# Reading the first layer's shifted copies straight from a padded input, and running its first unit of filters one image at a time

## The chip, the cores and the metric

The kernel runs on one core of one Trainium2 chip. The metric is the device time of one execution in microseconds (us). A core has five engines that run side by side, each in its own program order: TensorE (PE, matrix products; PEld is its weight load), VectorE (DVE), ScalarE (ACT), GpSimd (POOL) and SyncE (SP, which here only issues DMA transfers). They wait for one another through semaphores.

## The reference, cut to what matters

The input x has shape (4, 32, 32, 16): four images, 32x32 positions, 16 channels. Four layers follow, each adding its result to x:

```python
x = x + conv(gn(x), M0, W0, G0)          # layer 0
x = x + conv(gn(x), M1, W1, G1)          # layer 1
x = x + interval(gn(x), ...)             # layer 2, not touched here
x = x + conv(gn(x), M3, Wp3, G3)         # layer 3

def gn(v, G=8, eps=1e-5):                # groups of 2 channels, over the whole image
    g = v.reshape(B, H, W, 8, 2)
    m = mean(g, axis=(1, 2, 4)); s = var(g, axis=(1, 2, 4))
    return ((g - m) / sqrt(s + eps)).reshape(v.shape)

def conv(v, M, W, G):                    # G: (32, 32, 3, 3, 16, 16): own 3x3 filters per position
    first   = einsum('ijyx,byxc->bijc', M, v)
    shifted = conv3x3(v, kern)           # 1024 positions x 16 filters, each over the whole image
    diff    = relu(v[:, None, None] - shifted)
    second  = einsum('ijyx,bijyxc->bijc', W, diff)
    return first - second
```

For every position (i, j) and filter f a 3x3 convolution over 16 channels is made of the whole image, and what comes out is weighted and summed. The 1024 positions are eight chunks of 128; in a chunk, one filter and one image are one *step*: 128 outputs (positions of the chunk) times 1024 pixels, with 9 x 16 = 144 products each. The nine shifts (taps) of the image, 16 channels each, are the rows of the right-hand operand; they are spread over three *slots*: slot 0 holds taps 0 to 3, slot 1 taps 4 to 7, slot 2 tap 8. The upper and the lower half of the image lie in partitions 0 to 63 and 64 to 127.

The convolution is linear in its input, but the padding must be zero after the normalization, not before it.

## The kernel before: the parts that are touched

The four images are two groups of two (`GB` = 2). Phases run over (group 0, layer 0), (group 1, layer 0), (group 0, layer 1) and so on, six in all; while a phase runs, a generator `behind` slips the next phase's preparation between its steps. Instructions go to the engines in the order in which they are written.

The input of a phase is prepared by `before_conv`: normalize, transpose to channels on partitions, write to a padded image `xs` in device memory, read back 24 shifted copies.

```python
def group_norm(g, name, dst):            # on X[g]: 128 positions x 8 x 32 (image, channel)
    part = sums(X[g]) ; yield 2          # DVE
    m = mean_of(part) ; yield 1          # PE, a product with a constant matrix
    ...                                  # subtract, square, sum, PE, ACT sqrt, DVE reciprocal
    nc.vector.tensor_tensor(dst, xc, rstd, mult); yield 2

def before_conv(g, layer):
    yield from group_norm(g, f"c{g}{layer}", xn)
    ...                                  # two PE transposes of xn, ACT copy to xt
    for t in range(4):                   # xt -> xs, the padded image in device memory
        (nc.scalar if t % 2 else nc.sync).dma_start(inner[:, t], xt[...])
    yield 2
    for slot, row, tap in [(2, row, 8) for row in range(4)] + [(tap // 4, tap % 4, tap) for tap in range(8)]:
        for h in range(2):
            off = (HI * h + tap // 3) * HP + tap % 3
            r0 = 64 * h + C * row
            (nc.scalar, nc.sync)[at % 2].dma_start(          # 16 partitions x 2 images x 542
                im[g][r0 : r0 + C, slot, :, :RUN], xsv[:, :, off : off + RUN])
            at += 1
    yield 9
    halve(im9[g], im[g][:, 2], low_x)        # ACT: slot 2 rounded for the tap-8 product
    yield 2
    halve_rest(im9[g], im[g][:, 2], low_x)   # DVE
```

The weights come in *units* of eight filters (1.5 MB each, tile `raw`, four buffers). `prep` subtracts 1 from one tap's weight (so that the step yields shifted minus v) on POOL and makes the slot-2 weights `W9` on ACT; `prep_rest` finishes `W9` on DVE.

```python
load_raw(0); load_chunk(0)               # first instructions of the program, after the load of X[0]
...
start = before_conv(*phases[0]); ...     # all of it runs before the first step
prep(0); prep_rest(0)

def conv_layer(phase, behind):
    for t in range(NT):                  # 8 chunks
        for f in range(C):               # 16 filters
            u = n * NU + f // FU         # unit of eight filters
            if f % FU == 1: prep(u + 1); load_raw(u + 3)
            if f % FU == 4: prep_rest(u + 1)
            if f == 2: load_chunk(n + 1)
            for b in range(GB):          # 2 images: one step each
                ps = bank_pair(...)      # PSUM, three pairs of banks
                for slot in range(3):
                    for h in range(2):
                        nc.tensor.matmul(ps[:, h, :], lhsT=w[:, f % FU, :], rhs=v[:, :, :H], ...)
                nc.vector.scalar_tensor_tensor(junk, ps, 0.0, chunks[n], op0=min, op1=mult,
                                               accum_out=acc[...])
                wait -= 1
                if wait <= 0: wait = next(behind, 1 << 20)

def behind(phase):
    if phase == 0:
        load_raw(1); load_raw(2)
        nc.scalar.dma_start(X[1], x[1]); zeros(1); yield 1
        yield from constants()
    ...                                  # before_conv of the next phase, first_term
    if phase == 0: yield from first_term(g, layer)
```

Of the kernel before, what the change touches and what calls it, by code (L numbers as in the profile page):

```python
# [8 lines left out]
F32 = mybir.dt.float32  # L9
F32R = mybir.dt.float32r  # L10
AF = mybir.ActivationFunctionType
ALU = mybir.AluOpType
AX = mybir.AxisListType

P = 128
B, H, C = 4, 32, 16
NG = 2
GB = B // NG
GC = GB * C
NL = 3  # L20
NP = H * H
NT = NP // P
HP = H + 2
# [11 lines left out]


@with_exitstack
def net_kernel(ctx: ExitStack, tc: tile.TileContext, x, convs, iv_w, iv_b, out):

# [16 lines left out]
    def bank_pair(name):  # L58
        return psum.tile([P, 2, 512], F32, tag="ps", name=name)

    def bank(name):
        return psum.tile([P, 512], F32, tag="one", bufs=2, name=name)
# [3 lines left out]
    n_chunks = len(phases) * NT  # L66

    X = [const.tile([P, NT, GC], F32, name=f"X{g}") for g in range(NG)]
    nc.scalar.dma_start(X[0], x[0])


    raws, units, chunks = {}, {}, {}
# [1 line left out]
    def load_raw(u):  # L74
        if u < n_chunks * NU:
            n = u // NU
            raws[u] = wpool.tile([P, 3, FU, P], F32, tag="raw", bufs=4, name=f"raw_{u}")
            nc.sync.dma_start(raws[u], convs[phases[n // NT][1]][2][n % NT, u % NU])

    def load_chunk(n):  # L80
        if n < n_chunks:
            t = n % NT
            chunks[n] = wpool.tile([P, NP], F32, tag="WT", name=f"WT_{n}")
            nc.sync.dma_start(chunks[n], convs[phases[n // NT][1]][1][t * P : (t + 1) * P, :])

    load_raw(0)
    load_chunk(0)


    mean_w = const.tile([P, P], F32, name="mean_w")  # L90
# [19 lines left out]
    def halve(dst, src, mask):  # L110
        nc.scalar.activation(dst, src, AF.Copy, scale=mask[:, 1:2])  # L111

    def halve_rest(dst, src, mask):
        nc.vector.scalar_tensor_tensor(  # L114
            dst, src, mask[:, 0:1], dst.bitcast(F32), op0=ALU.mult, op1=ALU.add
        )
# [1 line left out]
    xs = [dram.tile([GC, NPP], F32, name=f"xs{g}") for g in range(NG)]  # L118
    zero = const.tile([P, HP], F32, name="zero")
    xt = [const.tile([P, 2, ROWS, HP], F32, name=f"xt{g}") for g in range(NG)]  # L120
    im = [const.tile([P, 3, GB, PITCH], F32, name=f"im{g}") for g in range(NG)]
    im9 = [const.tile([P, GB, PITCH], F32R, name=f"im9{g}") for g in range(NG)]

    def zeros(g):

        nc.gpsimd.memset(xt[g], 0.0)
        nc.gpsimd.memset(im[g][:, 2], 0.0)
        for y in (0, HP - 1):
            nc.gpsimd.dma_start(xs[g][:, y * HP : (y + 1) * HP], zero[:GC])

    nc.gpsimd.memset(zero, 0.0)
    zeros(0)

    def prep(u):

        if u >= n_chunks * NU:
            return
        raw = raws.pop(u)
        f0 = u % NU * FU
        nc.gpsimd.tensor_tensor(  # L140
            raw[:, 1], raw[:, 1],
            pick[:, f0 : f0 + FU].unsqueeze(2).to_broadcast([P, FU, P]),
            ALU.subtract,
        )
        W9 = wpool.tile([P, FU, P], F32R, tag="W9", name=f"W9_{u}")
        halve(W9, raw[:, 2], low_w)
        units[u] = (raw, W9)

    def prep_rest(u):
        if u in units:  # L150
            raw, W9 = units[u]
            halve_rest(W9, raw[:, 2], low_w)

# [44 lines left out]
    def before_conv(g, layer):  # L200
        xn = work.tile([P, NT, GC], F32, tag="xn", bufs=2, name=f"xn_{g}_{layer}")
        xns[g] = xn
        yield from group_norm(g, f"c{g}{layer}", xn)

        ps = bank(f"ps_t{g}{layer}")
        for m in range(2):
            nc.tensor.transpose(  # L209
                ps[:, m * P : (m + 1) * P],  # L210
                xn[:, 4 * m : 4 * m + 4, :].rearrange("p t m -> p (t m)"),
                ident,
            )
        yield 1
        nc.scalar.copy(
            xt[g][:, :, :, 1 : 1 + H],
            ps[:, : 2 * P].rearrange("p (m r x) -> p m r x", m=2, x=H),
        )
        inner = xs[g][:, HP : HP + H * HP].rearrange("p (m t n) -> p t m n", m=2, t=4)
        for t in range(4):  # L220
            (nc.scalar if t % 2 else nc.sync).dma_start(
                inner[:, t],
                xt[g][GC * t : GC * (t + 1)].rearrange("p m r x -> p m (r x)"),
            )
        yield 2
        xsv = xs[g].rearrange("(b c) n -> c b n", b=GB)
        at = 0
        for slot, row, tap in [(2, row, 8) for row in range(4)] + [
            (tap // 4, tap % 4, tap) for tap in range(8)
# [4 lines that stand above are left out]
                (nc.scalar, nc.sync)[at % 2].dma_start(  # L234
                    im[g][r0 : r0 + C, slot, :, :RUN], xsv[:, :, off : off + RUN]
                )
                at += 1
        yield 9
        halve(im9[g], im[g][:, 2], low_x)
        yield 2  # L240
        halve_rest(im9[g], im[g][:, 2], low_x)
# [215 lines left out]
    def conv_layer(phase, behind):  # L457

        g, layer = phases[phase]
        wait = 0  # L460
        imv = im[g].rearrange("p s b (y x) -> p s b y x", x=HP)
        im9v = im9[g].rearrange("p b (y x) -> p b y x", x=HP)
        acc = work.tile([P, NT, GC], F32, tag="acc", bufs=2, name=f"acc_{phase}")
        for t in range(NT):
            n = phase * NT + t
            for f in range(C):
                u = n * NU + f // FU
                if f % FU == 1:
                    prep(u + 1)
                    load_raw(u + 3)  # L470
                if f % FU == 4:
                    prep_rest(u + 1)
                if f == 2:
                    load_chunk(n + 1)
                W, W9 = units[u]
                for b in range(GB):


                    ps = bank_pair(f"pc_{n}_{f}_{b}")
                    for slot in range(3):  # L480
                        for h in range(2):
                            r = slice(64 * h, 64 * h + 64)
                            w, v = (W9[r], im9v[r, b]) if slot == 2 else (W[r, slot], imv[r, slot, b])
                            nc.tensor.matmul(  # L484
                                ps[:, h, :],
                                lhsT=w[:, f % FU, :],
                                rhs=v[:, :, :H],
                                start=slot == 0,
                                stop=slot == 2,
                            )  # L490

                    col = b * C + f
                    junk = work.tile([P, NP], F32, tag="junk", name=f"junk_{n}_{col}")
                    nc.vector.scalar_tensor_tensor(  # L494
                        junk,
                        ps.rearrange("p h n -> p (h n)"),
                        0.0,
                        chunks[n],
                        op0=ALU.min,
                        op1=ALU.mult,  # L500
                        accum_out=acc[:, t, col : col + 1],
                    )
                    wait -= 1
                    if wait <= 0:
                        wait = next(behind, 1 << 20)
            nc.vector.tensor_tensor(X[g][:, t], X[g][:, t], acc[:, t], ALU.add)  # L506
        for _ in behind:
            pass

    def behind(phase):  # L510
        g, layer = phases[phase]
        if phase == 0:
            load_raw(1)
            load_raw(2)
            nc.scalar.dma_start(X[1], x[1])
            zeros(1)
            yield 1
            yield from constants()
        if phase + 1 < len(phases):
            g1, layer1 = phases[phase + 1]  # L520
            if layer1 == 2:
                yield from interval_layer(g1)
            yield from before_conv(g1, layer1)
            yield from first_term(g1, layer1)
        if phase == 0:
            yield from first_term(g, layer)
        if phase == len(phases) - 1:
            nc.sync.dma_start(out[1 - g], X[1 - g])

    start = before_conv(*phases[0])  # L530
    next(start)
    v = ident.rearrange("p (h q c) -> p q c h", h=2, q=4)
    nc.vector.tensor_reduce(pick, v[:, 0], axis=AX.X, op=ALU.add)
    low_w = rows_mask("low_w", ident.rearrange("p (h w k) -> p w h k", h=2, w=2)[:, 1:2])
    low_x = rows_mask("low_x", ident.rearrange("p (g x k) -> p x g k", g=4, x=2)[:, 1:2])
    for _ in start:
        pass
    prep(0)
    prep_rest(0)
    for phase in range(len(phases)):  # L540
        conv_layer(phase, behind(phase))
    nc.sync.dma_start(out[1], X[1])
# [63 lines left out]
```

## Time and profile before

| | |
|---|---|
| time, median of 3 runs | 3120.36 us (3120.36 to 3121.54) |
| span in the profile | 3119.8 us |
| PE busy | 3089.7 us, 99% |
| DVE busy | 2100.3 us, 67% |
| POOL, ACT busy | 289.2 us (9%), 147.2 us (5%) |
| chain that ended last | PE 99%, DMA 1%, everything else under 0.5% each |

The profile is read as follows. The page gives each engine's busy time and the chain of work that ended last, followed back from the last instruction: at each point, what the next thing was waiting for. The timeline lists instructions in order of time (start, duration, engine, line of the kernel, operation, tile written and tiles read; in brackets how long the engine was idle before and what ended that). `pc` is the PSUM tile of a step, `junk` its evaluation on DVE, `im` the shifted copies, `raw` the weights, `ps_mc` and `ps_vc` the two small products of the group normalization. "SPq" and "ACTq" are the DMA-issuing sides of these engines. The windows view gives, for each stretch of time, the busy time of PE, PEld, DVE, ACT and POOL with instruction counts, the granted PE clock, the DMA engines' busy share and GB/s.

### The profile page before, as it was taken

The page shows a single profiled execution, that of the slowest core. Times are in us where ns is not written, and L with a number is a line of the kernel's source. Part 1 is how long each engine was busy: PE and PEld are TensorE (multiplying, and loading weights), DVE is VectorE, ACT ScalarE, POOL GpSimd, SP SyncE. Part 2 cuts the span into 40 slices and gives each one's busy share as a digit, 9 for nine tenths or more (in the row PEclk, how much of TensorE's full clock was granted, in tenths as well). Part 3 has the DMA queues.
Part 4 walks back from the last instruction along what each step waited for, and adds up shares of the span by engine and source line. Part 5 has one row for each costly group of instructions (what it writes and reads, how often), then busy time and mean ns, then how long its engine had stood idle before and what let it go on. Part 6 is the DMA issues. An engine that isn't in the chain of part 4 may idle for free.

```text
span 3119.8 us, 37923 instructions
## 1 busy us (share of the span) xinstructions
PE 3089.7 (99%) x15792; PEld 1568.0 (50%) x15792; DVE 2100.3 (67%) x3348; ACT 147.2 (5%) x159; POOL 289.2 (9%) x173
## 2 busy tenths in 40 slices
PE   6999999999999999999999999999999999999999
PEld 4444455444444444444446654444664444444444
DVE  4656666666666666666677766667776666666666
ACT  0000000000000000000000000000100000000000
POOL 2000000000000000000013300002230000000000
PEclk9999999999999999999999999999999999999999
DMA  4322111321111231211111132121113211111100
GB/s 144 123 102 75 48 68 48 125 75 66 50 62 60 69 124 48 75 48 68 48 70 52 48 118 75 48 75 48 68 48 103 97 48 70 48 72 51 67 28 2
DMA packets 32462, 215.21 MB, mean 69 GB/s; under 512 B 5665, under 2 KB 7713, under 8 KB 18465
## 3 DMA queue, kind: packets, MB, share of 16 engines
q1 hardware_dynamic: 27168, 207.02, 18.4%
q10 hardware_dynamic: 4992, 5.74, 0.9%
q8 instruction: 124, 2.03, 0.3%
q14 instruction: 50, 0.40, 0.0%
q0 software_dynamic: 128, 0.02, 0.0%
HBM read 211.64 MB, written 1.12 MB: 68 GB/s over the span
## 4 chain that ended last, share of the span: by engine, by line
PE 99%; DMA 1%; DVE 0%; ACTq 0%; issue 0%; ACT 0%
PE pc L484 97%; PE pf L255 1%; PE pfs L263 0%; DMA im<-xs 0%; PE ps_l L386 0%; DMA X<-in_x 0%; PE ps_r L397 0%; PE ps_l L384 0%; PE ps_t L209 0%; PE ps_vc L174 0%; PE ps_iv L341 0%; DMA xs<-xt 0%; PE ps_mc L174 0%; DVE xc_c L184 0%; ACTq L234 0%; DVE junk L494 0%
## 5 line engine op out<-in xcount | busy, mean ns | idle before, releaser
L484 PE MATMUL pc<-im,raw 64*128 64x512 f32 x12288 | 2920.4, 590 | 13.2 <-DMA im<-xs 13.2
L494 DVE SCALAR_TENSOR_TENSOR junk<-pc,WT 128x1024 f32<-128x1024 f32 x1536 | 1880.0, 1224 | 990.4 <-PE pc L484 986.6
L484 PEld LDWEIGHTS pc<-im,raw 64*128 64x128 f32 x12288 | 1237.2, 186 | 1137.5 <-issue 746.6
L484 PE MATMUL pc<-im,W 64*128 64x512 f32 x3072 | 1293.2, 803 | 0.0
L484 PEld LDWEIGHTS pc<-im,W 64*128 64x128 f32 x3072 | 321.1, 186 | 355.6 <-issue 343.5
L140 POOL TENSOR_TENSOR raw<-raw,pick 128x1024 f32<-128x1024 f32 x96 | 182.0, 1898 | 2278.5 <-DMA raw<-in_g 2216.9
L111 ACT ACTIVATE W<-raw,low_w 128x1024 fp32r<-128x1024 f32 x96 | 110.3, 1149 | 2198.0 <-PE pc L484 2170.1
L494 DVE DVE_READ_ACCUMULATOR junk<-pc,WT 128x1 f32 x1536 | 127.6, 83 | 0.0
L114 DVE SCALAR_TENSOR_TENSOR W<-raw,low_w,W 128x1024 fp32r<-128x1024 f32 x96 | 122.9, 1280 | 0.0
L417 POOL TENSOR_TENSOR dp_b<-ft_b,rt_r 128x1089 f32<-128x1089 f32 x16 | 39.1, 2449 | 101.6 <-ACT ft_b L410 51.5
L417 POOL TENSOR_TENSOR dp_a<-ft_a,rt_r 128x1089 f32<-128x1089 f32 x16 | 37.2, 2327 | 79.9 <-DVE s_a L424 50.2
L255 PE MATMUL pf<-MT,xn 128*32 128x512 f32 x192 | 23.1, 598 | 0.0
L424 DVE TENSOR_REDUCE s_b<-dp_b 128x33 f32<-128x1089 f32 x16 | 20.5, 1283 | 0.0
L424 DVE TENSOR_REDUCE s_a<-dp_a 128x33 f32<-128x1089 f32 x16 | 20.5, 1282 | 0.0
L114 DVE SCALAR_TENSOR_TENSOR im<-im,low_x,im 128x1088 fp32r<-128x1088 f32 x6 | 9.1, 1523 | 14.6 <-DMA im<-xs 14.6
L259 ACT COPY fs<-pf 128x512 f32<-128x512 f32 x12 | 7.0, 586 | 240.1 <-PE pf L255 240.1
L330 POOL TENSOR_SCALAR xn<-xn 128x256 f32<-128x256 f32 x2 | 1.7, 856 | 151.0 <-DVE xn L195 151.0
L506 DVE TENSOR_TENSOR X<-X,acc 128x32 f32<-128x32 f32 x48 | 13.6, 283 | 1.6
L263 PEld LDWEIGHTS pfs<-stack,fs 128*128 128x128 f32 x96 | 11.2, 191 | 3.4 <-issue 3.4
L361 DVE TENSOR_TENSOR pp<-pp 64x1024 f32<-64x1024 f32 x10 | 12.1, 1213 | 0.0
L366 DVE TENSOR_TENSOR pp<-pp 64x1024 f32<-64x1024 f32 x10 | 12.1, 1213 | 0.0
L255 PEld LDWEIGHTS pf<-MT,xn 128*32 128x32 f32 x192 | 5.0, 109 | 14.1 <-issue 14.1
(81 smaller groups left out, 160.1 us busy)
## 6 DMA issues: line engine op xcount, KB each, us to landing
raw<-in_g SPq DMA_DIRECT2D x96, 1536.0 KB, 6.6
WT<-in_w SPq DMA_DIRECT2D x48, 512.0 KB, 6.3
MT<-in_mt SPq DMA_DIRECT2D x12, 2048.0 KB, 8.3
im<-xs SPq DMA_DIRECT2D x72, 67.8 KB, 3.2
im<-xs ACTq DMA_DIRECT2D x72, 67.8 KB, 3.3
xs<-xt SPq DMA_DIRECT2D x12, 34.0 KB, 1.7
xs<-xt ACTq DMA_DIRECT2D x12, 34.0 KB, 1.8
X<-in_x ACTq DMA_DIRECT2D x2, 128.0 KB, 5.1
```

Of the source, the lines that this page charges most:

```text
L111: nc.scalar.activation(dst, src, AF.Copy, scale=mask[:, 1:2])
L114: nc.vector.scalar_tensor_tensor(dst, src, mask[:, 0:1], dst.bitcast(F32), op0=ALU.mult, op1=ALU.add)
L140: nc.gpsimd.tensor_tensor(raw[:, 1], raw[:, 1], pick[:, f0 : f0 + FU].unsqueeze(2).to_broadcast([P, FU, P]), ALU.subtract,)
L255: nc.tensor.matmul(ps[32 * j : 32 * j + 32, :], lhsT=xn[:, pt, :], rhs=mt[:, pt, :], start=pt < 4, stop=pt >= 4, tile_position=(0, 32 * j),)
L263: nc.tensor.matmul(ps[:, GC * t : GC * (t + 1)], lhsT=fs[:, t // 4, t % 4 * P : (t % 4 + 1) * P], rhs=stack, start=True, stop=True,)
L361: nc.vector.tensor_tensor(pp[k][:, :H, M:], a[:, :H, M:], a[:, s : H + s, M:], ALU.max)
L366: nc.vector.tensor_tensor(pp[k][:, :H, M:], a[:, :H, M:], a[:, :H, M - s : M - s + H], ALU.max)
L417: nc.gpsimd.tensor_tensor(t, ft[:, i, :].unsqueeze(1).to_broadcast([P, T1, T1]), rt, ALU.add,)
L424: nc.vector.tensor_reduce(s[:, i - 1, :], last, axis=AX.X, op=ALU.max)
L484: nc.tensor.matmul(ps[:, h, :], lhsT=w[:, f % FU, :], rhs=v[:, :, :H], start=slot == 0, stop=slot == 2,)
L494: nc.vector.scalar_tensor_tensor(junk, ps.rearrange("p h n -> p (h n)"), 0.0, chunks[n], op0=ALU.min, op1=ALU.mult, accum_out=acc[:, t, co ...
L506: nc.vector.tensor_tensor(X[g][:, t], X[g][:, t], acc[:, t], ALU.add)
```

## The change

Only the first phase (group 0, layer 0) is started differently. The host gives two further forms of the two images of group 0: `xq`, the same numbers as 128 partitions of 256 (for the statistics), and `xp`, channels on partitions and already padded by a ring of zeros. The 24 shifted copies are read from `xp` at the very start, before the statistics are known, and are normalized in place; where the padding has thereby become non-zero it is multiplied by zero (masks `keep_...`). The round trip over transposes and `xs` falls away for this phase. The copies, the first unit's weights and the first unit's steps are split so that image 0 and the first two filters can begin before the rest is there. The normalization of X[0] in the usual form is still needed for the first term and runs behind the steps.

```diff
-    nc.scalar.dma_start(X[0], x[0])
+    XQ = const.tile([P, 256], F32, name="XQ")
+    nc.scalar.dma_start(XQ, xq)
...
-    load_raw(0)
+    def load_copies(b, slot):                # 8 copies, 16 partitions x 542, of one image
+        for h in range(2):
+            for row in range(4):
+                tap = min(4 * slot + row, 8)
+                ...
+                (nc.scalar if h and b == 0 else nc.sync).dma_start(
+                    im[0][r0 : r0 + C, slot, b, :RUN], xpv[:, b, off : off + RUN])
+    F0 = 2
+    raws[0] = wpool.tile([P, 3, FU, P], F32, tag="raw", bufs=4, name="raw_0")
+    load_copies(0, 0)
+    nc.sync.dma_start(raws[0][:, :, :F0], convs[0][2][0, 0][:, :, :F0])
+    load_copies(0, 2)
+    load_copies(0, 1)
     load_chunk(0)
+    nc.sync.dma_start(raws[0][:, :, F0:], convs[0][2][0, 0][:, :, F0:])
+    for slot in (2, 0, 1):
+        load_copies(1, slot)
...
-            for f in range(C):
+            steps = [(f, b) for f in range(C) for b in range(GB)]
+            if n == 0:
+                steps.sort(key=lambda s: (s[0] // FU, s[1]))     # eight steps of image 0, then of image 1
+            for at, (f, b) in enumerate(steps):
-                if f % FU == 1:
+                if at % (FU * GB) == 2:
+                    load_raw(u + 3)
+                if at % (FU * GB) == (8 if u == 0 else 2):
                     prep(u + 1)
-                    load_raw(u + 3)
-                if f % FU == 4:
+                if at % (FU * GB) == (12 if u == 0 else 8):
                     prep_rest(u + 1)
...
         if phase == 0:
             load_raw(1)
             load_raw(2)
+            yield from rest_of_start()
             nc.scalar.dma_start(X[1], x[1])
...
-    start = before_conv(*phases[0])
+    pairs = ...; own = ...; to_rows = ...; to_own = ...; rows = ...      # from the identity, on DVE
+    keep = {...}                                                         # six masks, two DVE instructions each
+    s1 = sum of XQ                                # DVE
+    mean_own = to_own.T @ s1                      # PE, DVE copy
+    XQ -= mean_own; s2 = sum of XQ * XQ           # DVE
+    var = to_rows.T @ (own * s2); rstd0 = sqrt(var + eps)    # DVE, PE, ACT
+    mean0 = to_rows.T @ (own * s1); rstd0 = 1 / rstd0        # DVE, PE, DVE
+
+    def normal(eng, b, slots):
+        for slot in slots:
+            v = im[0][:, slot, b, :RUN]
+            eng.tensor_scalar(v, v, mean0[:, b : b + 1], rstd0[:, b : b + 1], op0=subtract, op1=mult)
+            ...                                   # slots 0, 1: three small multiplications by keep; slot 2: two memsets
+
+    prep(0, 0, F0)
+    normal(nc.vector, 0, [0, 2])
+    prep_rest(0, 0, F0)
+    normal(nc.gpsimd, 0, [1])
+    halve(im9[0][:, 0], im[0][:, 2, 0], low_x)
+    halve_rest(im9[0][:, 0], im[0][:, 2, 0], low_x)
+    prep(0, F0, FU)
+
+    def rest_of_start():                          # from behind(0), after the first step
+        nc.sync.dma_start(X[0], x[0])
+        prep_rest(0, F0, FU)
+        normal(nc.gpsimd, 1, [2, 0, 1])
+        yield 4
+        halve(im9[0][:, 1], im[0][:, 2, 1], low_x)
+        yield 1
+        halve_rest(im9[0][:, 1], im[0][:, 2, 1], low_x)
+        nc.gpsimd.memset(zero, 0.0)
+        zeros(0)
+        xns[0] = work.tile(...)
+        yield from group_norm(0, "c00", xns[0])
```

## The prediction, made before the changed kernel had run

> **What bounds the kernel now.** I read the page first: PE is busy 99% of the span, and only the first of its 40 slices (78 us each) is not full.
>
> ```profile
> PE 3089.7 (99%) x15792; PEld 1568.0 (50%) x15792; DVE 2100.3 (67%) x3348; ACT 147.2 (5%) x159; POOL 289.2 (9%) x173
> ...
> PE   6999999999999999999999999999999999999999
> ```
>
> All that a change of the start can win lies in that slice: 6 tenths of 78 us busy leaves some 30 us. The chain of waits in order of time, for the first 60 us, shows of what they are made (start, duration, what):
>
> ```profile
> 0.80 7.32 DMA X<-in_x
> ...
> 15.25 2.10 DMA xs<-xt
> ...
> 18.86 3.92 DMA im<-xs
> ...
> 22.79 3.53 DMA im<-xs
> ...
> 26.34 3.31 DMA im<-xs
> ...
> 29.89 27.40 PE pc L484 x113
> 57.29 0.32 PE ps_mc L174 x2
> ```
>
> The load of X takes 7.3 us, the normalization up to 14.8, the write to xs up to 17.35, the copies up to 29.65; then PE is the chain. The copies come as three waves, because the program gives its DMAs eight semaphores in turn and the ninth waits for the first. The timeline of the same stretch gives the steps' beat:
>
> ```profile
> 32.62 1.23 DVE L494 SCALAR_TENSOR_TENSOR junk<-pc,WT 128x1024 f32<-128x1024 f32 x1 [1.92 <-PE pc L484]
> ...
> 35.75 1.23 DVE L494 SCALAR_TENSOR_TENSOR junk<-pc,WT 128x1024 f32<-128x1024 f32 x1 [1.90 <-PE pc L484]
> ...
> 37.72 1.23 DVE L494 SCALAR_TENSOR_TENSOR junk<-pc,WT 128x1024 f32<-128x1024 f32 x1
> ...
> 47.52 1.23 DVE L494 SCALAR_TENSOR_TENSOR junk<-pc,WT 128x1024 f32<-128x1024 f32 x1 [0.73 <-PE pc L484]
> ```
>
> First evaluation at 32.62, second 3.13 later, then one in 1.96 us; the eighth at 47.52. A step that shares PE with ps_mc takes longer: the evaluations at 57.32 and 59.81 are 2.49 apart, 0.53 more. Last, how fast the DMAs go (windows view, then single issues from the DMA view, issued at 27.18, 28.98 and 29.38 on SP and at 26.91 on ACT):
>
> ```profile
> 20.00:23.00 3.00, 0.00 (x0) 0.00 (x0) 0.00 (x0) 0.00 (x0) 0.00 (x0) 1.00 1.09 168
> ...
> 34.00:38.00 4.00, 4.00 (x22) 2.95 (x20) 2.18 (x6) 0.93 (x1) 2.14 (x4) 1.00 1.00 416
> ```
> ```profile
> raw<-in_g SPq DMA_DIRECT2D x1, 1536.0 KB, 6.6
> ```
> ```profile
> raw<-in_g SPq DMA_DIRECT2D x1, 1536.0 KB, 8.6
> ```
> ```profile
> raw<-in_g SPq DMA_DIRECT2D x1, 1536.0 KB, 11.9
> ```
> ```profile
> X<-in_x ACTq DMA_DIRECT2D x1, 128.0 KB, 3.0
> ```
>
> The shifted copies keep the DMA engines full (share 1.09) at only 168 GB/s; weights move at 416. Three units issued close together on SP land at 33.8, 37.5 and 41.3, one every 3.75 us, in order; a small load on ACT's queue, just ahead of them, takes 3.0.
>
> **What the skill says.** (1) The Trainium skill, "DMA: Bandwidth & Descriptors", section "Queues, rings and completion order": each DMA engine consumes one queue's descriptors in ring order and takes turns between queues. The three landings agree; it decides where X lands below. (2) Same page, "Rules for kernel authors": transfers under 64 KB pay mostly overhead. The copies of 67.8 KB already show it (2.3 us for the first, alone, against 0.44 for each further one in a full wave); the new ones have 33.9 KB. (3) "GPSIMD Engine Reference", "Key points": GpSimd shares its SBUF interfaces with VectorE instructions that have two SBUF inputs or run in a 2-port mode. The trace agrees: xc_c took 1.45 us beside a POOL subtraction, and 0.43 in layer 2. (4) "VectorE: DVE Perf Modes", "Mode 2×_2P": fp32 tensor_scalar reaches two elements a cycle. No tensor_scalar of such a size is in this trace, so I take 0.4 to 0.7 us for 542 elements.
>
> **The change, part by part.** Times are from the start of the profile.
>
> *Masks.* DVE makes them from the identity, ready at 1.37: reductions of 128 elements are 0.28 (mask2), of 32 to 64 0.18 to 0.21, a tensor_scalar of one element 0.15. Three large ones (0.84), three products (0.6), six keep pairs at about 0.3 (1.8), pick, low_w and low_x (0.9), with gaps some 4.6 us: DVE is free at about 6. XQ (128 KB, no weights ahead of it) lands near 3, so the masks set the start of the statistics.
>
> *Statistics.* Sum 0.42, PE 0.62, copy 0.17, subtract 0.35, squares 0.5, product 0.15, PE 0.62, sqrt 0.28, reciprocal 0.2: 3.3 us, to 9.5. There is a second chain to the sqrt: on ACT, the table load (1.28) now stands behind twelve copies, the last of which waits two landings: about 2.9, 5.3, 7.6, issue to 8.0, table to 9.3, sqrt to 9.6. Both give 9.7 for rstd0.
>
> *Copies of image 0.* 24 at 0.22 us each (half of 0.44) are 5.3 us of DMA, but in chains of eight semaphores with some 2.1 us each: SP's slowest is first copy (2.9), first part of raw (0.39 MB, to about 6.3), a slot-2 copy (8.7), a slot-1 copy (issued 8.8, landed 11). So slot 0 is there by 5.5, slot 2 by 9, slot 1 by 11.
>
> *Normalizing.* DVE: slot 0, 0.5 plus three small ones 0.5, to 10.7; slot 2 to 11.4; ACT im9 (half of 1.20 plus overhead) 0.7, DVE's part 0.8 (half of 1.35, plus): 12.9 to 13.4. POOL: slot 1 from 11 on. A tensor_scalar there costs 856 ns for 256 elements and 2982 for 1089, so about 1.6 for 542, and 0.7 for the three small ones: 13.4. The last two matmuls of the first step then give the first evaluation near 15.3 (1.7 us from W9 to the evaluation before: 30.94 to 32.62). That is 17.3 us ahead of 32.62.
>
> *Rest of unit 0.* WT and raw's rest are issued at 9.3 and 9.7 and land by 12.3 and 15.2. Step 3, near 20, needs W9 and POOL's subtraction of it (1.45): 17, in time.
>
> *Image 1.* SP issues its 24 copies after raw's rest. The eighth waits for that rest (15.2); the next sixteen follow at 0.30 each: the last leaves at 20.5. POOL normalizes three slots at 2.3 until 25; step 9 needs them near 31. Hidden.
>
> *X[0].* This is what I expect to end last. raw_1, raw_2 and X[0] go to SP behind those copies, at 20.6 to 21.5, in one queue. raw_1 lands 6.5 later (27.1), raw_2 3.75 after (30.9), X at 31.3. The changed program's order puts the sum over X[0] (0.42, DVE) ahead of the seventh evaluation, and ps_mc (PE) ahead of the ninth step. PE has done eight steps at 15.3 + 3.1 + 6 x 1.96 = 30.2, and would go on at 31.3 + 0.42 + 0.53 = 32.3; before, the ninth step began at 47.2. Of 17.3 us some 14.9 are left.
>
> *Given back.* ps_vc also moves between steps: 0.5. The DVE work of this normalization (some 2.5 us over 15 steps) fits: DVE has 0.65 us free in each step, and PSUM three pairs. Sum: 14.9 - 0.5 = 14.4 to 14.9, so about **3105.5 us**. Steady steps, 1536 of them, do not change.
>
> **Rivals.**
> - *X[0] is early*, because the copies or the weights go faster, and no wait takes its place. For: ACT's X took 3.0. Against: here it stands behind two units on SP. Gain then 17.3 - 1.0 = 16.3: 3104.
> - *Image 1 or X[0] is late.* The eighth semaphore's chain runs through every large load; 2 to 4 us more in raw's rest shift everything on SP. POOL would also shift. Gain 11 to 12: 3109.
> - *The start itself is late by 3 us or more*, by DVE and POOL holding each other (3), or slow small instructions. The wait for X[0] then partly hides it: 1.8 us of lateness cost nothing. 3107.
> - *Copies choke the weights*: 168 against 416 GB/s in the first 20 us. Counted in the chains; were it worse, step 3 would wait for raw's rest: 3108.
>
> **Range and chances.** The best case (start at 13.5, X not felt) is 3101.5; two of the late ones together give 3110. The range is 3101.5 to 3110. A gain of 2% would need 62 us, twice the whole start; a loss of 2% would need steady steps to change. Faster 0.5%, within 2% 99%, slower 0.5%.
>
> **What would show it.** First evaluation at 15 to 16; rstd0 at 9.7, with ACT's table load just before; POOL's slot 1 and DVE's im9 within 1 us of each other as the last things before step 1; a wait of PE of 1 to 3 us after eight steps, put down to part_mc and behind it to the landing of X[0] near 31; then 1.96 again. If PE goes from step 8 to 9 without a gap, the X step is wrong; if the first evaluation lies after 18, the sum of the start is.

## The result and the profile after

The changed kernel takes 3120.84 us (median of 6 runs, 3120.30 to 3121.97), the kernel before, run beside it, 3120.57 us (6 runs, 3119.03 to 3121.54): ratio 1.0002, 95% interval 0.9989 to 1.0015. The predicted gain of 15 us is not there. The page answers to the lines shown of before:

```profile
PE 3100.2 (99%) x15796; PEld 2024.2 (65%) x15796; DVE 2105.1 (67%) x3384; ACT 147.7 (5%) x161; POOL 302.2 (10%) x190
...
PE   7999999999999999999999999999999999999999
```

The first slice is fuller, 7 tenths instead of 6, as meant. But PEld is busy for 2024.2 us where it was 1568.0, with four more instructions in 15796, and PE for 10.5 us more. Four small products cannot be that much work. Next, the timeline of DVE (start, duration, operation; in brackets the idle time before and what ended it), with the evaluations of the first steps:

```profile
18.73 1.22 DVE L519 SCALAR_TENSOR_TENSOR junk<-pc,WT 128x1024 f32<-128x1024 f32 x1 [3.00 <-PE pc L509]
...
21.28 1.22 DVE L519 SCALAR_TENSOR_TENSOR junk<-pc,WT 128x1024 f32<-128x1024 f32 x1 [0.39 <-PE pc L509]
...
23.24 1.22 DVE L519 SCALAR_TENSOR_TENSOR junk<-pc,WT 128x1024 f32<-128x1024 f32 x1 [0.73 <-PE pc L509]
...
36.49 0.42 DVE L189 TENSOR_REDUCE part_mc<-X 128x16 f32<-128x256 f32 x1 [5.43 <-DMA X<-in_x]
36.83 1.22 DVE L519 SCALAR_TENSOR_TENSOR junk<-pc,WT 128x1024 f32<-128x1024 f32 x1
```

The first evaluation comes at 18.73 instead of 32.62: 13.9 us were won. Then the sum over X[0] stands and waits until 36.49. I call the *lead* of a step how much earlier its evaluation starts than in the profile of before:

| evaluation | lead of after, us |
|---|---|
| 1st | 13.90 |
| 33rd | 6.77 |
| 128th | 6.04 |
| 515th | 3.81 |
| 1027th | 1.67 |
| 1536th, the last | -0.79 |

So there are two losses: 7.1 us within the first 33 steps, and 6.8 us spread over everything from step 128 to the end. (The 0.7 between are the transposes of group 1, which stand before step 33 in one kernel and after it in the other.) The profile of before is of an execution of 3121.54 us, 1 us over the median of the runs beside after, so a lead taken against it can be high by about as much.

**The first loss.** The chain of waits of after, in order of time (start, duration, what):

```profile
3.12 4.41 DMA raw<-in_g
...
10.23 7.53 DMA raw<-in_g
17.77 0.31 SPq L101
...
25.43 0.42 SPq L101
...
25.89 0.42 SPq L81
...
26.36 0.43 SPq L81
...
26.83 9.63 DMA X<-in_x
...
36.49 0.43 DVE part_mc L189
...
36.96 0.61 PE ps_mc L196 x2
37.57 11.05 PE pc L509 x40
```

It does not run through the first step at all. It runs through SP: the rest of raw holds the eighth semaphore until 17.77, then SP issues copies of image 1 at 0.42 us and a gap of 0.04 each, then two weight units, then X[0], which is issued at 26.83 and lands 9.63 us later. PE has eight steps done by 33.0 and stands still until ps_mc:

```profile
36.96 0.61 PE L196 MATMUL ps_mc<-part_mc,mean_w 128*128 128x16 f32 x2 [3.96 <-DVE part_mc L189]
```

What that costs besides is in the windows view (busy time of PE, PEld, DVE, ACT, POOL; then the granted PE clock, DMA share, GB/s):

```profile
33.00:37.00 4.00, 0.04 (x2) 0.04 (x1) 0.51 (x2) 0.58 (x1) 3.97 (x7) 0.98 1.02 427
37.00:43.60 6.60, 6.60 (x18) 3.35 (x20) 4.03 (x8) 0.00 (x0) 1.59 (x2) 0.50 0.52 212
44.00:50.00 6.00, 6.00 (x34) 2.90 (x32) 4.50 (x9) 0.28 (x1) 0.00 (x0) 1.00 0.00 1
```

4 us without a product, and then 6.6 us at a clock of 0.50: 18 matmuls where a stretch of 6.0 us at full clock has 34. By the clock records of the trace the half clock lasts from 36.83 to 43.66, so by estimate some 3.4 us of work (half of 6.83) are lost on top of the wait of 3.96: 7.4 in all.

**The second loss.** In the timeline a step of steady work is ten records of PE: eight with raw, two with W9 (`W`), of which one is for the upper and one for the lower half of the partitions. PE's timeline at 2700 us, before first:

```profile
2699.66 1.88 PE L484 MATMUL pc<-im,raw 64*128 64x512 f32 x8
2700.98 0.81 PE L484 MATMUL pc<-im,W 64*128 64x512 f32 x2
2701.62 1.88 PE L484 MATMUL pc<-im,raw 64*128 64x512 f32 x8
2702.94 0.81 PE L484 MATMUL pc<-im,W 64*128 64x512 f32 x2
```

and after:

```profile
2699.51 0.80 PE L509 MATMUL pc<-im,W 64*128 64x512 f32 x1
2699.91 1.02 PE L509 MATMUL pc<-im,raw 64*128 64x512 f32 x3
2700.36 0.81 PE L509 MATMUL pc<-im,W 64*128 64x512 f32 x1
2700.58 1.45 PE L509 MATMUL pc<-im,raw 64*128 64x512 f32 x5
2701.47 0.80 PE L509 MATMUL pc<-im,W 64*128 64x512 f32 x1
2701.87 1.02 PE L509 MATMUL pc<-im,raw 64*128 64x512 f32 x3
2702.33 0.81 PE L509 MATMUL pc<-im,W 64*128 64x512 f32 x1
```

Before, the two W products of a step run together (x2). After, they run one by one, 0.85 us apart (2699.51, 2700.36), and the next pair begins at 2701.47, 1.96 after the first. The two halves no longer march in step. Take the starts of all W products from the trace, one half against the other, in the long stretches without other products on PE. Before, the second half (by the program's order the lower one) lags by at most 0.010 us, and both take 1.9600 us a step. After, in every such stretch, the second half takes 1.9667 us, and the lag grows by 6.7 ns a step up to 1.31 us, where the first half slows to 1.9667 too. At the next product over the whole array the lag is paid: between the W products of the 259th and 260th step, say, 3.48 us pass in the upper half, and 2.49 in before. This also fits PEld's 65%: weight loads that lay on top of one another now lie apart. (Near the products of the interval layer, in steps 818 to 847, the halves are 0.33 to 0.34 us apart in both kernels, and there the distance does not grow, in after neither; why is open.)

Neither the products nor their order are changed in those stretches. What is changed is where their operands lie. The changed kernel has other tiles ahead of the image copies (`im`) and of the weights: by the compiled programs, im begins at byte 19584 of a partition instead of 22016, raw at 65824 instead of 62304.

### The profile page after: what moved, and what is told of

Its sections match the earlier page's. It is cut to its first block, busy times and chain, and to the rows that moved or that the text cites. A ratio compares the mean times of both kernels' runs of the same rounds, so it can differ in the third digit from the quotient of the medians.

```text
span 3120.3 us, 38037 instructions
## 1 busy us (share of the span) xinstructions
PE 3100.2 (99%) x15796; PEld 2024.2 (65%) x15796; DVE 2105.1 (67%) x3384; ACT 147.7 (5%) x161; POOL 302.2 (10%) x190
## 4 chain that ended last, share of the span: by engine, by line
PE 99%; DMA 1%; SPq 0%; DVE 0%; issue 0%
PE pc L509 97%; PE pf L277 1%; DMA raw<-in_g 0%; PE pfs L285 0%; PE ps_l L408 0%; DMA X<-in_x 0%; SPq L101 0%; PE ps_r L419 0%; DMA im<-in_xp 0%; PE ps_l L406 0%; PE ps_iv L363 0%; PE ps_mc L196 0%; PE ps_vc L196 0%; PE ps_t L231 0%; DVE junk L519 0%
## 5 line engine op out<-in xcount | busy, mean ns | idle before, releaser
L509 PE MATMUL pc<-im,raw 64*128 64x512 f32 x12288 | 3007.6, 590 | 4.8 <-DVE im L643 4.2
L509 PEld LDWEIGHTS pc<-im,raw 64*128 64x128 f32 x12288 | 1708.4, 186 | 762.1 <-issue 424.3
L509 PE MATMUL pc<-im,W 64*128 64x512 f32 x3072 | 1820.9, 803 | 0.0
L509 PEld LDWEIGHTS pc<-im,W 64*128 64x128 f32 x3072 | 492.6, 186 | 275.9 <-issue 219.9
L164 POOL TENSOR_TENSOR raw<-raw,pick 128x1024 f32<-128x1024 f32 (+1 forms) x97 | 182.2, 1880 | 2240.9 <-DMA raw<-in_g 2150.3
L138 ACT ACTIVATE W<-raw,low_w 128x1024 fp32r<-128x1024 f32 (+1 forms) x97 | 110.6, 1140 | 2199.2 <-PE pc L509 2164.7
L141 DVE SCALAR_TENSOR_TENSOR W<-raw,low_w,W 128x1024 fp32r<-128x1024 f32 (+1 forms) x97 | 123.1, 1269 | 0.0
L285 PEld LDWEIGHTS pfs<-stack,fs 128*128 128x128 f32 x96 | 11.2, 191 | 3.4 <-issue 3.4
L383 DVE TENSOR_TENSOR pp<-pp 64x1024 f32<-64x1024 f32 x10 | 12.1, 1212 | 0.0
L388 DVE TENSOR_TENSOR pp<-pp 64x1024 f32<-64x1024 f32 x10 | 12.1, 1212 | 0.0
L408 PE MATMUL ps_l<-r,f 64*128 64x264 f32 x48 | 12.1, 391 | 0.0
```

Of the source, the lines that this page charges most:

```text
L141: nc.vector.scalar_tensor_tensor(dst, src, mask[:, 0:1], dst.bitcast(F32), op0=ALU.mult, op1=ALU.add)
L164: nc.gpsimd.tensor_tensor(raw[:, 1, at:to], raw[:, 1, at:to], pick[:, f0 + at : f0 + to].unsqueeze(2).to_broadcast([P, to - at, P]), ALU.s ...
L383: nc.vector.tensor_tensor(pp[k][:, :H, M:], a[:, :H, M:], a[:, s : H + s, M:], ALU.max)
L388: nc.vector.tensor_tensor(pp[k][:, :H, M:], a[:, :H, M:], a[:, :H, M - s : M - s + H], ALU.max)
L408: nc.tensor.matmul(o, lhsT=wf[q], rhs=r[:, QI * q : QI * (q + 1), :], start=hidden is None and q == 0, stop=q == NQ - 1,)
```

## The experiments

Two theories: the first loss is X[0] behind the weights on SP (rival: image 1's normalization on POOL would hold the ninth step anyway); the second is the tiles' places (rivals: the new order of the steps, or the chip's own drift over a run). Times are medians, and ratios are against the kernel before, run beside each.

**e1: X[0] ahead of the weight units.**

```diff
     def behind(phase):
         if phase == 0:
+            nc.sync.dma_start(X[0], x[0])
             load_raw(1)
             load_raw(2)
...
     def rest_of_start():
-        nc.sync.dma_start(X[0], x[0])
```

> The changed kernel with the load of X[0] issued ahead of the weights raw_1 and raw_2 on the same queue; nothing else. Theory A (PE's gap after eight steps comes from X[0] standing behind two units of weights, and the slow clock for 6.8 us after it from that gap): X[0] lands near 28 instead of 36.5, PE goes on after its eighth step without a gap over 0.7 us, no second stretch of half clock, the 17th evaluation 7 us earlier, time 3120.8 - 7 = 3113 to 3114 us if the drift of the two halves stays. Rival B (the gap has another cause behind it: image 1's copies, POOL's normalization of them, or im9 are late as well): PE still waits 2 us or more at the ninth step, now for POOL or DVE im, gain under 4 us: 3117 to 3120.

Measured: 3114.1 us (before 3120.09), ratio 0.9982 (0.9974 to 0.9989). X[0] is issued at 26.32 and lands at 28.35; the DMA view has its landing time, after first, then e1:

```profile
X<-in_x SPq DMA_DIRECT2D x1, 128.0 KB, 9.6
```
```profile
X<-in_x SPq DMA_DIRECT2D x1, 128.0 KB, 2.0
```

and the chain of waits of e1 has PE without a gap through the first eight steps and beyond, and its clock records no 0.50 before the end of the program:

```profile
13.61 18.22 PE pc L509 x72
31.83 0.33 PE ps_mc L196 x2
32.16 8.04 PE pc L509 x40
```

The lead at step 33 is 15.19, 8.4 more than in after (0.7 of that is the earlier first step of this profile; the rest is 4.0 of wait and 3.4 of half clock, within 0.4). The loss after step 128 is as in after: 14.46 falls to 7.64. So the first loss is X[0]'s place in the queue, image 1 on POOL is not behind it, and the second loss has another cause.

**e2: the changed kernel, its tiles back at the old places.** Two unused tiles; im is at 22016 again and raw at 70496, which is 8192 past the old place.

```diff
     nc.scalar.dma_start(XQ, xq)
+    pad1 = const.tile([P, 608], F32, name="pad1")
...
+    pad2 = const.tile([P, 560], F32, name="pad2")
     for phase in range(len(phases)):
```

> The changed kernel with two unused tiles that put im and im9 at the addresses they have in the kernel before (im0 at 22016 instead of 19584), and raw, WT, W9 and MT at the same addresses modulo 8192; the instructions and their order are the same. Theory C (the lower half's matmuls falling 6.7 ns behind in every step of the quiet stretches comes from where the new constants moved the tiles in SBUF): both halves take 1.9600 us a step in the quiet stretches, lag under 0.02 us, time 3120.8 - 6.8 = 3114 us. Rival D (it comes from the instructions, their waits or the moment at which a stretch begins, not from addresses): lag grows to 1.0 to 1.3 us as before, time 3120.8 within 1.

**e3: the kernel before, its tiles moved** by pads of 1440 and 1488 elements: im at 27776, raw at 74016.

> The kernel before with two unused tiles that give im, im9, raw, WT, W9 and MT the addresses modulo 8192 that they have in the changed kernel; nothing of the computation or its order is changed. Theory C (addresses): the lower half falls behind by 6.7 ns a step in the quiet stretches, up to 1.0 to 1.3 us of lag, and the time rises by some 7 us to 3127. Rival D: both halves stay at 1.9600, 3120.5 within 1.

Measured: e2 3114.55 us, ratio 0.9982 (0.9976 to 0.9989); e3 3127.06 us, ratio 1.0023 (1.0014 to 1.0031). The page of e2, then of e3, in its first line:

```profile
PE 3092.6 (99%) x15796; PEld 1561.2 (50%) x15796; DVE 2104.6 (68%) x3384; ACT 147.7 (5%) x161; POOL 301.5 (10%) x190
```
```profile
PE 3096.8 (99%) x15792; PEld 1957.8 (63%) x15792; DVE 2099.8 (67%) x3348; ACT 147.2 (5%) x159; POOL 289.2 (9%) x173
```

Two tiles that nobody reads take PEld from 65% to 50% and all drift away (lag at most 0.008 us in the long stretches, lead 6.04 at step 128 and 5.94 at the end); two such tiles in the kernel before, whose instructions are otherwise its own, bring PEld to 63% and the drift with it, and cost 7 us. Neither the order of the steps nor the chip's own drift is needed.

**e4: e1 and e2 together.**

> The changed kernel with both edits, X[0] ahead of the weights and the tiles at the old addresses. If A and C hold, the two losses are separate and add up: 3120.8 - 7 - 6.8 = 3107 us. If D holds and A: 3113.5. If only C: 3114.

Measured: 3107.95 us (4 runs, 3106.52 to 3108.71), ratio 0.9961 (0.9946 to 0.9976). The lead is 14.76 at step 128 and 14.66 at the end. The two losses add, and with both away the profile has what the change was to bring. By the medians it is less, 12.1 us: the profile of e4 is of the shortest of its four executions (3106.52), that of before of one 1 us over its median.

**e5 to e10 and e12: which place?** All but the last are the kernel before with unused tiles; e5 moves im alone by 128 bytes (raw by 8192), e6 the weights alone (880 elements), e9 both by small amounts, e10 the weights alone so that their distance to im is that of after. (The pads of e9 move im by 128 bytes and the weights by 192, not by 32 as its expectation below says.)

```diff
 e5  +  pad1 = const.tile([P, 32], F32)      +  pad2 = const.tile([P, 2016], F32)
 e6                                          +  pad2 = const.tile([P, 880], F32)
 e9  +  pad1 = const.tile([P, 32], F32)      +  pad2 = const.tile([P, 16], F32)
 e10                                         +  pad2 = const.tile([P, 1488], F32)
 e12 (the changed kernel)                    +  pad  = const.tile([P, 16], F32)
```

> The kernel before, with im and im9 alone moved by 128 bytes a partition (im0 at 22144, the place modulo 256 that it has in the changed kernel); raw, WT, W9 and MT at their old addresses modulo 8192. Theory C1 (the place of the streamed operand im, im9 makes the lower half fall behind): lag 1.3 us in the quiet stretches, 3127 us. C2 (the place of the weights raw, W9 does): no lag, 3120. C3 (their places relative to one another count): lag, 3127, and e6 has it too.

> The kernel before, with raw, WT, W9 and MT alone moved (raw at 65824, exactly where the changed kernel has it), im and im9 where they were. C1: no lag, 3120 us. C2: lag 1.3 us in the quiet stretches, 3127. C3: lag, 3127.

> The kernel before, with the image copies moved up by 128 bytes and the weight tiles by 32 bytes in all (two unused tiles of 32 and 16 elements); whole kibibytes and the distance between the two are nearly as before. What is disputed is which part of the two places decides whether the lower half of the array falls behind. Low-bits theory (the places within a few hundred bytes decide, for both tiles together): the lower half takes 1.9667 us a step in the quiet stretches and its lag grows to over 1 us; time 3124 to 3127. Distance theory (how far the weights lie from the images decides): both halves 1.9600, lag under 0.02; time 3119.5 to 3121.5.

> The kernel before, with only the weight tiles moved, up by 5952 bytes, so that they lie exactly as far from the images (46240 bytes) as in the changed kernel and in the kernel before with both moved, while the images stay where they were. Distance theory: the lower half of the array falls behind in four or five quiet stretches (1.9667 us a step), time 3125 to 3128. Theory of absolute places (only the pair of places counts): the drift is as with the weights moved alone by 3520 bytes, in one stretch or none, time 3120 to 3122.

| kernel | im at | raw at | raw modulo 128 | drifting stretches of five | lost after step 128, us | time, us | ratio (95%) |
|---|---|---|---|---|---|---|---|
| before | 22016 | 62304 | 96 | 0 | 0 | 3120.57 | 1 |
| after | 19584 | 65824 | 32 | 5 | 6.8 | 3120.84 | 1.0002 (0.9989 to 1.0015) |
| e2 | 22016 | 70496 | 96 | 0 | 0.1 | 3114.55 | 0.9982 (0.9976 to 0.9989) |
| e3 | 27776 | 74016 | 32 | 4 | 6.4 | 3127.06 | 1.0023 (1.0014 to 1.0031) |
| e5 | 22144 | 70496 | 96 | 0 | 0.0 | 3120.59 | 1.0002 (0.9993 to 1.0010) |
| e6 | 22016 | 65824 | 32 | 1 | 0.9 | 3121.17 | 1.0004 (0.9996 to 1.0013) |
| e9 | 22144 | 62496 | 32 | 4 | 6.4 | 3126.59 | 1.0023 (1.0014 to 1.0032) |
| e10 | 22016 | 68256 | 32 | 4 | 6.1 | 3125.80 | 1.0020 (1.0012 to 1.0028) |

(The stretches are those of at least 85 steps without other products: steps 94 or 109 to 258, 309 to 514, 565 to 770, 941 to 1026, 1197 to 1535. The loss is the fall of the lead between the 128th and the last evaluation.)

After e5 and e6 neither tile alone seemed to do it, which left the distance between the two as a theory, and e10 by itself came out as that theory forecast. e9 ends it: a shift by 64 bytes against one another, with everything else nearly where it was, brings the whole drift. Lined up, the table has one column that goes with the drift: no kernel whose weights begin 96 bytes past a multiple of 128 drifts, and every kernel with 32 does, in one stretch at least. That rule was made after the runs, so it was put to the test on a kernel with im at a place that no run without drift had had:

> The changed kernel with one unused tile of 16 elements, which moves the weight tiles up by 64 bytes (from 65824 to 65888) and leaves the images where they are (19584). In every run so far in which the lower half of the array fell behind, the weights began 32 bytes past a multiple of 128; in every run without it, 96 bytes past one; the images always began on such a multiple. Theory that the weights' place within 128 bytes decides: both halves take 1.9600 us a step, lag under 0.02 in every quiet stretch, time 3113 to 3115, about 6.5 us below the changed kernel, with its start (first evaluation 18.7, wait before the ninth step 4 us) unchanged. Rival, that higher bits or the two places together decide and the pattern so far is chance: the drift stays in some of the stretches, time 3117 to 3121.5.

Measured: 3114.15 us (3112.58 to 3115.71; before 3120.12), ratio 0.9981 (0.9974 to 0.9988); lag at most 0.010 us in the long stretches, lead 5.92 at step 128 and 5.95 at the end. PE's timeline of e12 at 2700 us:

```profile
2699.58 1.88 PE L509 MATMUL pc<-im,raw 64*128 64x512 f32 x8
2700.90 0.81 PE L509 MATMUL pc<-im,W 64*128 64x512 f32 x2
```

The W products are back together. 16 unused elements per partition are worth 6 us. How much drift 32 brings is not settled by this column: e6 has it in one stretch of five, with im where e10 has it in four. Nor do the runs say which of the tiles matters, for raw, W9, WT and MT all moved by the same amount; and as the images began on a multiple of 128 in every run, the weights' own place can't be told from their place relative to the images.

**e7 and e8: what ends the start.** In after, the chain that ends last before the first step is one of two: ACT's table load, behind twelve copies, or POOL's slot 1. e7 is e4 with a square root of one element between ACT's copies, so that the table is loaded while ACT waits for landings. e8 is e7 with image 0's slot 1 on DVE and slot 2 on POOL.

```diff
 e7  +    nc.scalar.activation(rstd0[:, 0:1], eps, AF.Sqrt, bias=eps)   # after load_copies(0, 2)
 e8  -    normal(nc.vector, 0, [0, 2])           +    normal(nc.vector, 0, [0, 1])
 e8  -    normal(nc.gpsimd, 0, [1])              +    normal(nc.gpsimd, 0, [2])
```

> The version with X[0] ahead and the old addresses (3107.95 us), with the table load of ACT moved in front of the last four copies by a sqrt of one element that nothing uses. Theory E (the start ends with POOL: the last slot-1 copy at 11.3 and then POOL's 2.7 us and three small ones): rstd0 is there at 9.5 instead of 11.1, DVE's slot 0 is done 1.5 us earlier, the first evaluation moves by less than 0.5 us, 3107.5 to 3108. Rival F (ACT's table load holds the start): first evaluation 1.5 us earlier, 3106.4.

> As e7, and for image 0 DVE normalizes slots 0 and 1 and POOL slot 2 (two memsets in place of three small multiplications). Theory E: slot 1 is done near 13.2 and im9 near 14.5, so the first evaluation comes near 15.5 instead of 18.0; but POOL still finishes image 1 near 31, so the ninth step, now due near 29.7, waits about 1 us for im: gain 1 to 2 us, 3106 to 3107. Rival F: no more than e7 gained.

Measured: e7 3109.1 us, ratio 0.9964 (0.9951 to 0.9977); e8 3105.5 us (4 runs, 3105.19 to 3106.91), ratio 0.9955 (0.9940 to 0.9970). In e7 the table is loaded at 5.53 and the reciprocal is made at 10.40 instead of 11.07, but nothing is won: first evaluation 19.53, against 17.99 in e4. POOL's timeline of e7 shows why:

```profile
13.05 2.47 POOL L633 TENSOR_SCALAR im<-im,mean,rstd 128x542 f32<-128x542 f32 x1 [4.93 <-DVE im L638]
15.62 0.37 POOL L646 TENSOR_SCALAR im<-im,keep_left 128x16 f32<-128x16 f32 x1
15.95 0.35 POOL L646 TENSOR_SCALAR im<-im,keep_right 128x16 f32<-128x16 f32 x1
16.40 0.36 POOL L646 TENSOR_SCALAR im<-im,keep_bottom 128x32 f32<-128x32 f32 x1
```

POOL's slot 1 began only at 13.05. The bracket names DVE's L638, but what it had to wait for is a copy: ACT's twelfth, which the table load had pushed back to 9.68, behind the load of WT on SP (9.59), and which landed at 12.79 instead of 11.00. The 0.7 us won at the reciprocal were lost at the last landing, and PE's next products at 16.82 wait for POOL. With slot 1 on DVE, in e8, PE runs from 12.99 without a gap, 0.83 us ahead of e4 (13.82, also without one). DVE and PE of e8:

```profile
10.81 0.95 DVE L633 TENSOR_SCALAR im<-im,mean,rstd 128x542 f32<-128x542 f32 x1 [0.25 <-DMA im<-in_xp]
...
12.80 0.58 DVE L633 TENSOR_SCALAR im<-im,mean,rstd 128x542 f32<-128x542 f32 x1
```
```profile
12.99 19.10 PE pc L512 x72
32.09 0.33 PE ps_mc L199 x2
```

The second fence is the chain of waits: 72 of the 80 records of the first eight steps, and no wait up to ps_mc. The first evaluation is at 17.41, not near 15.5 as expected. The lead at the end is 14.30, and e4's is 14.66; but e8's profile is of the longest of its four executions (3106.91), e4's of the shortest. By the medians e8 is ahead by 2.4 us, and the intervals of the two ratios overlap. e8 has the lowest median of the study, and is not shown to be faster than e4.

**e11: e8 with three filters ahead in place of two** (`F0 = 3`), because I took the slow second step (2.98 us after the first) for a wait for the rest of raw.

> The version with the X load early, the old places, the table load early and the slots exchanged, with three filters of the first unit loaded ahead in place of two. There PE waited for the rest of the first unit (landed 18.06, its subtraction on POOL done 19.65). Theory that this rest is the next bound of the start: the first evaluation comes 0.3 to 1 us later (the first part of raw is half as large again), but the wait after the second filter's step goes, and steps 4 to 8 come 1 to 2 us earlier; at the end 1 us or more before the version with two filters, 3104 to 3105. Rival: the copies and this larger first part share the same DMA engines, so what the rest gains the start loses; equal to two filters within 0.7 us, 3105 to 3106.5.

Measured: 3107.12 us (3106.28 to 3107.29; before 3119.67), ratio 0.9960 (0.9945 to 0.9975); first evaluation 17.96, second 2.82 later, lead at the end 13.89. The premise was wrong, as e8's chain above, read properly, says: there is no wait there. PE's timeline of e8 has the cause in the durations:

```profile
15.78 1.41 PE L512 MATMUL pc<-im,W 64*128 64x512 f32 x1
...
19.44 0.80 PE L512 MATMUL pc<-im,W 64*128 64x512 f32 x1
```

The same product takes 1.41 us in the first step and 0.80 in the second: the first step runs at about half speed. The clock records of e8 begin only at 19.25, at 1.00, which is 6.3 us after the first of these products; before that the trace has none, and the windows view's 1.00 for the start stands for no record. How long this lasts differs between profiles. In e12 the records begin at 16.50, 3.0 us after the first of these products (13.54), and the product that took 1.41 takes 0.80 to 0.88 in the first step already:

```profile
16.33 0.88 PE L509 MATMUL pc<-im,W 64*128 64x512 f32 x1
...
16.50 0.80 PE L509 MATMUL pc<-im,W 64*128 64x512 f32 x1
```

The larger first part of e11 won nothing; its first evaluation is 0.55 us later than e8's, which is within the scatter of the start.

## Why the prediction failed, step by step

- **"Steady steps, 1536 of them, do not change."** This is the step that failed. It was true of the instructions, and it was the only part of the program that I did not look at, 99% of the time. They came to cost 6.8 us more because of where the tiles lie that they read: shown by e2, e3 and e12, each in its own direction. It is not the weights' new address alone: e6 has them exactly there, with the images at their old place, and loses 0.9. The sign "then 1.96 again" was too coarse for 1.9667 against 1.9600; PEld's share, 65% against 50%, shows it.
- **X[0]**: the mechanism was right, to the engine named in the wait (part_mc, behind it the landing of X), and its size was wrong. Predicted were a landing at 31.3 and a wait of 1 to 3 us (2.1 in the sum). It landed at 36.47. The terms: the rest of raw lands at 17.76, not 15.2; SP takes 0.42 + 0.04 for each copy, not 0.30, so that X is issued at 26.83 instead of 21.5; the landing then takes 9.63, as predicted (9.8). The wait of 3.96 was followed by 3.4 us of half clock that the sum did not have. The Trainium skill says in "TensorE: Matmul & The Clock Gate", section "Part 1: The HAM clock gate", that PE falls to half its clock after an idle window of about 3.4 us; the trace agrees (0.50 after 4.0 us). The prediction did not apply it to this wait. With e1's one moved line the term is gone.
- **The start**: predicted 15.3, measured 18.73 (17.3 to 19.0 over the profiles of this start). rstd0 was ready at 11.2 instead of 9.7: the statistics themselves were faster than said (the variances stood in PSUM at 8.0), but ACT's twelfth copy was issued at 9.02 to 9.45, and the table load, in ACT's order behind it, ended at 10.76. POOL's slot 1 took 4.4 us instead of 2.3:

```profile
11.58 2.68 POOL L630 TENSOR_SCALAR im<-im,mean,rstd 128x542 f32<-128x542 f32 x1 [3.29 <-DMA im<-in_xp]
14.36 0.47 POOL L643 TENSOR_SCALAR im<-im,keep_left 128x16 f32<-128x16 f32 x1
14.80 0.36 POOL L643 TENSOR_SCALAR im<-im,keep_right 128x16 f32<-128x16 f32 x1
15.24 0.71 POOL L643 TENSOR_SCALAR im<-im,keep_bottom 128x32 f32<-128x32 f32 x1
```

  The 1.6 us for 542 elements were interpolated from tensor_scalars of before; the small ones, 16 or 32 elements, cost 0.36 to 0.71 us each, not the 0.23 that went into the sum.
- **The rival "start late" was right that X hides it**: in e12 the first evaluation came at 17.34, 1.4 earlier than in after, but PE then stood still for 6.06 us before ps_mc, and the lead at step 33 was no greater (6.51 against 6.77).
- **Right**: the copies of image 0 (last landed 11.32, predicted 11); image 1 on POOL hidden (done at 31.66, not 25; e1 has no wait for it); the rest of raw in time for the third step; and no wait for DVE or PSUM in e1's chain between the first step and ps_vc (40.20). The sum of gains less what is given back, 14.4 to 14.9, is what e4's profile shows (14.66 to 14.76), though by partly cancelling errors: the first step is 2.7 us later than said, the X wait is absent. There is luck in it besides. By the times, e4 wins 12.1 us, 7.5 to 16.8 by its interval; the prediction was worked from a profile whose first evaluation, at 32.62, is the latest of the six with the old start (the others 30.59 to 32.31), and e4's profile is of its shortest execution.
- **The range** was made from the rivals alone, and all of them lay in the first 40 us. The chance of "within 2%" held, as every kernel here is within 0.5%.

## What to carry to other kernels

When a change adds or removes tiles, compare the addresses of what the steady loop reads, and in the profile the weight loads' busy time and whether paired products still stand together (x2); if they don't, try a pad of 64 bytes before looking for anything else. Follow a small load that sits in a queue behind large ones to its landing with the measured issue time of everything ahead of it, and ask what PE's clock does if PE stands still for as long as the 4.0 us seen here. Take the lead of one profile over another only beside the times of both executions. Moving such a load by one line (e1) and the pad (e12) were each worth some 6 us, where the whole rebuilt start without them had come to nothing.

## What the runs showed of the hardware

- Two halves of the array, fed by the same stream of products on partitions 0 to 63 and 64 to 127, can run apart by 6.7 ns in a step of 1.96 us, and whether they do goes with where the weight tiles begin: at 96 bytes past a multiple of 128 in none of five long stretches (before, e2, e5, e12), at 32 bytes in five (after), four (e3, e9, e10) or one (e6). The Trainium skill's "SBUF — State Buffer", section "Operand start alignment", says which addresses are legal and that its runs timed nothing; these runs time it. Why the place matters, and why e6 drifts in one stretch only, is open.
- After 4.0 us without a product PE's clock was 0.50 for 6.8 us (36.83 to 43.66), which by estimate added 3.4 us to the wait. In e12, with 6.06 us without a product, it was 0.50 from 33.57 to 43.81, 6.5 us of it while products ran again.
- A copy of 16 partitions x 542 elements takes SP 0.42 us to issue and 0.04 between two; 17 of them held SP from 17.77 to 25.85 in after.
- A tensor_scalar of 542 fp32 elements with two operands per partition takes POOL 2.2 to 3.0 us and DVE mostly 0.56 to 0.62. DVE took 0.95 in e8, 1.02 in e12 and 1.05 in e4, where it began 0.13, 0.05 and 0.04 us after one on POOL, but 0.56 in after where it began 0.10 us ahead of POOL's (11.48), and 0.56 again in the middle of it (13.21). For 16 elements POOL takes mostly 0.35 to 0.47, DVE mostly 0.23.
- The start of one and the same first part scatters by 1 to 2 us between profiles (first evaluation 30.6 to 32.6 with the old start), so that differences of that size can't be read from one profile. It goes with the clock: in the six profiles with the old start the lead at the ninth evaluation is the smaller the later the clock records begin, from 2.50 us (e10, records from 30.83) over 1.76, 1.53 and 1.43 (e9, e3, e6: 32.42, 33.79, 33.92) to 0 (before, 34.81) and -0.03 (e5, 35.19).
